# Buffers moved from the normalised tokens to the first projection's output in a windowed-attention and convolution kernel

## The chip, the cores and the metric

The kernel runs on one core of a Trainium2 chip. The metric is the device time of one launch in microseconds (us). Three executions of the kernel before took 3268.4, 3279.0 and 3279.86 us, with a median of 3279.0 us. One more execution was profiled; it took 3272.91 us, and its instructions span 3271.1 us.

## The reference, cut to what matters

There are two layers. The first is a windowed-attention block on a 4 x 128 x 128 x 128 image (batch, channels, rows, columns), followed by a depthwise convolution; the second is a pair of quantised 3x3 convolutions.

```python
reg = x[:, :, ih, iw]                       # 9 x 9 overlapping regions of 16 x 16 pixels, step 14
y = _ln(tok, ln1_g, ln1_b);  q, k, v = jnp.split(y @ w_qkv, 3, axis=-1)
attn = softmax(einsum(q, k) * hd ** -0.5);  o = einsum(attn, v)       # 4 heads of 32 channels
tok = o @ w_out + b_out + tok
xf = merged                                  # regions added back, divided by how often a pixel is covered
y = _ln(xf, ln2_g, ln2_b) @ w_p0 + b_p0      # first projection: 128 -> 256 channels, two halves of 128
ym = conv_general_dilated(y, dw_k, 5 x 5, feature_group_count=256)
ym = gelu(batchnorm(ym));  y = gelu(ym) @ w_p2 + b_p2 + xf
# second layer: quantise, conv3x3, batchnorm, quantise, conv3x3, batchnorm, + identity
```

## The kernel before, in words

**Bands.** The first layer is worked through in 36 bands: for each of the four images, nine rows of regions, with nine regions in a band. A band has 14 new rows of pixels (16 in an image's last band), cut into two chunks of 8 and 6 rows. Band number t runs `attention(t)` over its nine regions; I call the time of one region a slot, slot 0 to slot 8. TensorE, ScalarE, VectorE and SyncE follow the order in which the code records their instructions; only GpSimd's order is left to a scheduler.

**What goes beside the attention.** In each slot the main loop records the scores of region j, the values of region j-1, and between them four lists of side steps that `beside(t)` hands out. Three kinds of side work run:

- `ln1_chunks`, for the next band: normalise two chunks of input pixels (chunks a1 and a2). Its steps are squares, variance, deviation, spread, second (steps 0 to 4) and four projections to queries and keys (steps 5 to 8, line 483).
- `post_chunks`, for the band before: output projection (steps 0 and 1, line 535), the second layer norm (steps 2 to 6) and four first projections (steps 7 to 10: both halves of the channels for each half of the chunk, line 551). Its chunks are b1 and b2. Each first projection reads normalised tokens `xn` on TensorE, is evicted by ScalarE with its bias into a tile `y` (line 556), and is stored to the DRAM tensor `y_d` in runs of 256 bytes.
- `conv_steps`, from band 10 on: the depthwise convolution of an image that is complete, one step at a time, reading `y_d` into `u` tiles and writing `cv_d` (lines 590, 623, 637).

**Buffers.** `xnp` (line 181) holds three tiles of normalised tokens, 4 KB in each partition. The spread step broadcasts the reciprocal deviations from DRAM into such a tile (`xn<-row`, line 401, on SyncE's DMA queue), the second step multiplies it by the tokens on VectorE (line 411), and the projections read it. `y2t` (line 194) holds two tiles of 2 KB for each half of the channels; a first projection takes the front tile of its half's list and puts it at the end, so ScalarE can write it only when the store issued two projections of that half earlier has landed.

**Order of transfers.** Nearly all transfers are issued from SyncE's queue in the recorded order. A store is recorded one step after the step that made it.

**Slots and lists.** From band 10 on, b1's four first projections stand in slot 8 and b2's four in slot 0 of the next band (the list `left`). In bands 0 to 9, where there is no convolution, a table `full` (line 929; nine entries, one for each slot, with `f` the list left over from the band before) spreads them otherwise: two in slot 8, three in slot 0 and three in slot 1 of the next band; chunk a2's last two key and query projections stand in slot 7. After the last band a tail finishes the last image: `beside(T)` runs the remaining chunks one after the other, and `conv_rest` the remaining convolution.

A second copy of both layers with a safer softmax stands behind a flag; the profiled execution does not enter it.

Of the kernel before, what the change touches and what calls it, by code (L numbers as in the profile page):

```python
# [8 lines left out]
F32 = mybir.dt.float32  # L9
# [5 lines left out]
P = 128  # L15
# [6 lines left out]
RB = 4  # L22
# [10 lines left out]
CW = P // 2  # L33
# [13 lines left out]
def layers(  # L47
# [52 lines left out]
    def vector(v, name):  # L100
        n = v.shape[0] // P
        t = const.tile([P, n], F32, name=name)
        nc.sync.dma_start(out=t, in_=v.rearrange("(h p) -> p h", p=P))
        return t
# [16 lines left out]
    g1, b1 = vector(ln1_g, "g1"), vector(ln1_b, "b1")  # L121
# [3 lines left out]
    g2, b2 = vector(ln2_g, "g2"), vector(ln2_b, "b2")  # L125
# [7 lines left out]
    with (  # L133
# [21 lines left out]
        for w in (wqkv, wp0.rearrange("p h m -> p (h m)")):  # L155
            n = w.shape[1]
# [18 lines left out]
    with ExitStack() as actx:  # L175
        pool = lambda name, bufs, **k: actx.enter_context(
            tc.tile_pool(name=f"{name}_{tag}", bufs=bufs, **k)
        )
        rp, op = pool("rp", 2), pool("op", 2)
        y2p = pool("y2p", 1)  # L180
        work, dev, xnp, xfp = pool("work", 1), pool("dev", 2), pool("xnp", 3), pool("xfp", 2)
        rowp = pool("rowp", 4, space=bass.MemoryType.DRAM)
        small = pool("small", 6)
        ps_s, ps_o, ps_m = (pool(n, k, space=PSUM) for n, k in (("ps_s", 1), ("ps_o", 1), ("ps_m", 3)))
# [3 lines left out]
        pool = lambda name, bufs: bctx.enter_context(tc.tile_pool(name=f"{name}_{tag}", bufs=bufs))  # L188
# [2 lines left out]
        att, attn_t, attn_v = pool("att", 2 if safe else 4), pool("attn_t", 2), pool("attn_v", 2)  # L191


        y2t = [[y2p.tile([P, RB, 2, CW], F32, name=f"y2_{h}{n}") for n in range(2)] for h in range(2)]

        stores = []
        xb, xr, yr, qs, kr, ob = {}, {}, {}, {}, {}, {}
# [264 lines left out]
        def ln1_chunks(t, sel=None):  # L462

            chunks = []
            for at, (r, n) in enumerate(row_blocks(t)):
                held = {}
                squares, variance, deviation, spread, scaled = normalise(
                    lambda r=r, n=n: xb[t, r][:, : n * P], n * P, sel
                )

                def second(r=r, n=n, at=at, held=held, scaled=scaled):
                    held["xn"] = scaled()
                    load_ahead(t, at)
                    for hh in range(2):
                        nc.gpsimd.tensor_copy(
                            yr[t][:, :, r + hh * n // 2 : r + (hh + 1) * n // 2, :],
                            windows(held["xn"][hh], n // 2),
                        )

                def project(m, hh, r=r, n=n // 2, held=held):  # L480
                    r = r + hh * n
                    pm = ps_m.tile([P, 512], F32, name="pm")
                    nc.tensor.matmul(  # L483
                        pm[:, : n * P], wqkv[:, m * P : (m + 1) * P], held["xn"][hh],
                        start=True, stop=True,
                    )
                    if m:
                        nc.scalar.copy(kr[t][:, :, r : r + n, :], windows(pm, n))
                    else:
                        nc.scalar.activation(  # L490
                            rows_of(qs[t], r, n), pm[:, : n * P], AF.Identity, bias=qb
                        )

                chunks.append(
                    [squares, variance, deviation, spread, second]
                    + [lambda p=project, m=m, hh=hh: p(m, hh) for hh in range(2) for m in range(2)]
                )
            return chunks
# [15 lines left out]
        def fetch(t, n):  # L514

            xr[t, n] = load_rows(rp, "xr", t, *finished(t)[n])
# [353 lines left out]
        def beside(t, sel=None):  # L870

            one = list(early) if t else ln1_chunks(1)
            early[:] = ln1_chunks(t + 2) if t + 2 < T else []
            two = post_chunks(t - 1, sel) if t else []
            had = len(todo)
            if t >= 2:
                b, i = bands[t - 2]
                if i == NR - 1 and b < B - 1:  # L880
                    todo.extend(conv_steps(b))
                    share[0] = NR if b < B - 2 else 5
                elif b == B - 1 and i == 4:
                    todo.extend(conv_steps(B - 1))
                    share[0] = 2
                elif b == B - 1 and i == 6:
                    todo.extend(conv_steps(B))
                    share[0] = 1

            fresh = len(todo) > had  # L890
            n = len(todo) // share[0] if fresh else -(-len(todo) // max(share[0], 1))
            conv = [todo.pop(0) for _ in range(n)]
            share[0] -= 1
            a1, a2 = one if one else ([None] * 9,) * 2
            b1, b2 = two if two else ([None] * 11,) * 2
            if t == T:
                return [
                    *conv, *left, *b1[:2], *b2[:2], b1[2], b1[3], b2[2], b2[3], b1[4], b2[4], b1[5], b2[5],
                    b1[6], *b1[7:], b2[6], *b2[7:],
                ]  # L900


            c = [[] for _ in range(NR)]
            d = [[] for _ in range(NR)]
            twice = len(conv) > NR
            for j in sorted((1, 3, 5, 7, 8, 4, 6, 2, 0)[: len(conv)]):
                c[j] = [conv.pop(0)]
                d[j] = [conv.pop(0)] if twice and j and conv else []
            x1 = lambda: fetch(t, 0)
            x2 = lambda: fetch(t, 1)  # L910
            f, left[:] = list(left), b2[7:]
            s1 = early[0][0] if early else None
            plan = [
                ([a1[1]], [], f, [*c[0], a1[2]]),
                ([], [a1[3], *c[1]], [], [a2[0]]),
                ([a2[1]], [a1[4]], b1[:2], [*c[2], a2[2]]),
                ([], [a2[3], *c[3]], [], [b1[2]]),
                ([b1[3]], [a2[4]], [*a1[5:], *b2[:2]], [*c[4], b1[4]]),
                ([], [b1[5], *c[5]], [], [b2[2]]),
                ([b2[3]], [b1[6]], a2[5:], [*c[6], b2[4]]),  # L920
                ([], [b2[5], x1, *c[7]], [], []),
                ([], [b2[6], x2], b1[7:], [*c[8], s1]),
            ]
            if t == 0:
                plan[0] = ([], [], [], [*c[0], *a1[:3]])
            if t <= NR:

                left[:] = [*b1[9:], *b2[7:]]
                full = (f[:3], f[3:], b1[:2], a1[5:7], a1[7:], b2[:2], a2[5:7], a2[7:], b1[7:9])
                plan = [(one, two, w, four) for (one, two, three, four), w in zip(plan, full)]  # L930
            return [(one, two, three, four + d[j]) for j, (one, two, three, four) in enumerate(plan)]

# [8 lines left out]
        todo, share, left, early = [], [0], [], []  # L941
# [14 lines left out]
        with nullcontext() if safe else tc.manual_schedule(engines=MANUAL):  # L956
# [5 lines left out]
            for t in range(T):  # L962
                flush(len(stores))
                scores, halves, values_in, values = attention(t)
                if t + 1 < T:
                    ln1_begin(t + 1)
                for j, side in enumerate(beside(t)):
                    scores(j)
                    if last:
                        last()  # L970
                    run(side[0])
                    halves(j)
                    if j == 0 and t:
                        post_begin(t - 1)
                    run(side[1])
                    if j % 2 == 0:
                        values_in(j)
                    run(side[2])
                    run(side[3])
                    last = lambda j=j, values=values: values(j)  # L980
# [9 lines left out]
            flush(len(stores))  # L990
            rest = conv_rest(len(units) - 1, pools[0], pools[0], pools[1])
            run(beside(T, selector(pools[0].tile([P, 4 * P], F32, name="sel"))))
            flush(len(stores))
            rest()
# [337 lines left out]
def conv_seq_kernel(tc: tile.TileContext, *args: bass.AP):  # L1332
    nc = tc.nc
    with tc.tile_pool(name="flag", bufs=1) as fp:
        flag = fp.tile([1, 1], mybir.dt.int32, name="flag")
        layers(tc, False, flag, *args)


        large = nc.values_load(flag[0:1, 0:1])
        with tc.If(large > 0):  # L1340
            layers(tc, True, flag, *args)
# [34 lines left out]
```

## Time and profile before

| quantity | value |
|---|---|
| median of three runs | 3279.0 us |
| profiled execution | 3272.91 us |
| its span | 3271.1 us |
| TensorE busy | 3100.5 us, 95% of the span |
| VectorE busy | 2019.6 us, 62% |
| ScalarE busy | 1990.9 us, 61% |
| GpSimd busy | 837.5 us, 26% |
| DMA queue of SyncE | 75.6% of 16 engines' span |

The share of busy time is an average over the whole kernel; how far one engine waits for another is seen in the waits of a stretch. TensorE's busy time also contains matmuls that run at a lower clock. I number the bands by the first score matmul of every ninth slot: band 10 begins at 513.3 us, band 28 at 1557.8 us, band 29 at 1622.7 us, and the last band at 2098.3 us. The tail lies from about 2206 to 2335 us, and the second layer after it.

### The profile page before, as it was taken

How to read it: one execution, taken by the hardware profiler on the slowest of the kernel's cores; microseconds unless marked ns; L12 is line 12 of the kernel's file. 1: busy time of each engine (PE TensorE's matmuls, PEld its weight loads, DVE VectorE, ACT ScalarE, POOL GpSimd, SP SyncE). 2: the span in 40 equal slices, each digit the busy share in tenths (PEclk: the TensorE clock that was granted, in tenths of full speed). 3: DMA queues.
4: the chain of work that ended last, by engine and by line, in shares of the span. 5: the costliest groups of instructions: out<-in, count | busy, mean ns of one | idle time of the engine just before them, and what ended most of it. 6: DMA issues, size and time to landing. Idle time of an engine off the chain costs nothing.

```text
span 3271.1 us, 75716 instructions
## 1 busy us (share of the span) xinstructions
PE 3100.5 (95%) x30954; PEld 1550.6 (47%) x30954; DVE 2019.6 (62%) x3249; ACT 1990.9 (61%) x2654; POOL 837.5 (26%) x1058
## 2 busy tenths in 40 slices
PE   8999999999999999999999998886899999999998
PEld 4555554454444544444444445554444444444343
DVE  5877887766766667676655565442455555666543
ACT  5777776777776776777656564532467777333443
POOL 3444443333333333333322232211111111000000
PEclk9999999999999999999999998876799999999999
DMA  3555677888886788886899989857899999452398
GB/s 81 150 165 158 170 186 182 193 208 198 212 197 164 182 202 205 201 211 164 194 204 206 206 196 204 195 158 191 260 356 357 358 360 295 148 166 66 105 359 309
DMA packets 809827, 680.65 MB, mean 208 GB/s; under 512 B 580918, under 2 KB 695935, under 8 KB 809471
## 3 DMA queue, kind: packets, MB, share of 16 engines
q1 hardware_dynamic: 798879, 669.17, 75.6%
q8 instruction: 247, 4.05, 0.5%
q0 software_dynamic: 1024, 3.93, 0.5%
q10 hardware_dynamic: 9568, 2.61, 0.4%
q14 instruction: 109, 0.89, 0.1%
HBM read 408.72 MB, written 270.79 MB: 208 GB/s over the span
## 4 chain that ended last, share of the span: by engine, by line
PE 79%; DMA 7%; ACT 4%; issue 4%; DVE 3%; SPq 2%; POOL 0%; ACTq 0%; DVEq 0%; POOLq 0%
PE pc L1150 19%; PE pm L590 9%; PE sc L773 9%; PE po L836 8%; PE pb L1208 7%; PE pm L483 7%; PE pm L551 5%; PE pm L759 4%; PE po L844 4%; PE pm L367 3%; PE pm L535 3%; DMA y_d<-y 2%; ACT pt L781 1%; DMA u<-y_d 1%; DMA xn<-row 1%
## 5 line engine op out<-in xcount | busy, mean ns | idle before, releaser
L856 DVE RECIPROCAL rd<-po 128x256 f32<-128x256 f32 x324 | 569.2, 1757 | 462.1 <-PE po L844 459.3
L1150 PE MATMUL pc<-q,wq 128*128 128x512 fp8e4 x3168 | 702.1, 381 | 14.3 <-DVE q L1162 14.3
L781 ACT ACTIVATE pt<-sc 128x1024 f32<-128x1024 f32 x648 | 628.1, 1024 | 133.6 <-PE sc L773 69.1
L791 POOL TENSOR_TENSOR sm<-pt 128x512 f32<-128x512 f32 x324 | 413.1, 1275 | 1059.3 <-ACT pt L781 735.4
L1150 PEld LDWEIGHTS <-wq 128*128 128x128 fp8e4 x3168 | 309.1, 98 | 417.7 <-issue 50.3
L773 PE MATMUL sc<-q,kr 32*128 32x256 f32 x5184 | 404.6, 415 | 18.5 <-ACT pt L781 18.3
L590 PE MATMUL pm<-u,w 40*32 40x504 f32 (+5 forms) x7680 | 370.3, 506 | 32.7 <-DMA u<-y_d 21.0
L773 PEld LDWEIGHTS sc<-q,kr 32*128 32x128 f32 x5184 | 250.0, 191 | 258.6 <-issue 166.9
L836 PE MATMUL po<-pt,v 128*32 128x256 f32 x5184 | 361.2, 398 | 6.8 <-DVE part L860 5.5
L637 ACT COPY c<-pm 128x512 f32<-128x512 f32 (+1 forms) x256 | 132.4, 563 | 264.1 <-PE pm L590 243.4
L551 PE MATMUL pm<-xn,wp 128*128 128x512 f32 (+1 forms) x576 | 249.7, 564 | 36.4 <-ACT y L556 35.6
L556 ACT ACTIVATE y<-pm,bp 128x512 f32<-128x512 f32 (+1 forms) x288 | 183.0, 641 | 149.7 <-DMA y_d<-y 88.3
L791 DVE TENSOR_TENSOR sm<-pt 128x512 f32<-128x512 f32 x324 | 243.6, 752 | 25.7 <-ACT pt L781 25.7
L483 PE MATMUL pm<-xn,wqkv 128*128 128x512 f32 (+1 forms) x576 | 248.5, 560 | 2.7 <-ACT v L764 2.0
L590 PEld LDWEIGHTS pm<-u,w 40*32 40x32 f32 x7680 | 148.5, 113 | 213.1 <-issue 154.1
L641 DVE BATCH_NORM_STATS2 st<-c 128x6 f32<-128x512 f32 (+2 forms) x320 | 160.7, 550 | 132.2 <-ACT c L637 131.7
L1208 PE MATMUL pb<-cv,wp 128*128 128x512 f32 x512 | 232.9, 599 | 7.1 <-ACT cv L1199 7.1
L836 PEld LDWEIGHTS po<-pt,v 128*32 128x32 f32 x5184 | 139.7, 111 | 180.6 <-issue 105.6
L844 PE MATMUL po<-sm,ones 128*32 128x256 f32 x2592 | 206.3, 389 | 1.2 <-issue 1.2
L1158 DVE BATCH_NORM_STATS2 st<-pc 128x6 f32<-128x512 f32 x256 | 165.6, 689 | 67.5 <-PE pc L1150 67.5
L759 PE MATMUL pm<-wqkv,yr 128*128 128x128 f32 x1296 | 193.1, 290 | 1.3 <-ACT c L637 1.3
L759 PEld LDWEIGHTS pm<-wqkv,yr 128*128 128x128 f32 x1296 | 158.7, 191 | 69.9 <-issue 44.4
(157 smaller groups left out, 3445.4 us busy)
## 6 DMA issues: line engine op xcount, KB each, us to landing
cv<-cv_d SPq DMA_DIRECT2D x64, 1024.0 KB
u<-y_d SPq DMA_DIRECT2D x234, 256.0 KB
cv_d<-c SPq DMA_DIRECT2D x192, 256.0 KB
y_d<-y SPq DMA_DIRECT2D x160, 256.0 KB
xn<-row SPq DMA_DIRECT2D x76, 512.0 KB
xfl<-xf_d SPq DMA_DIRECT2D x64, 512.0 KB
id_d<-y SPq DMA_DIRECT2D x64, 512.0 KB
idt<-id_d SPq DMA_DIRECT2D x64, 512.0 KB
```

What stands on the lines that cost most here:

```text
L483: nc.tensor.matmul(pm[:, : n * P], wqkv[:, m * P : (m + 1) * P], held["xn"][hh], start=True, stop=True,)
L551: nc.tensor.matmul(pm[:, : n * P], wp0[:, h, :], held["xn"][hh], start=True, stop=True)
L590: nc.tensor.matmul(outs[half][32 * q : 32 * q + 32, j, :, a:z], wt[hs, s, c, :], ut[hs, :, c, a + s - 1 : z + s - 1], start=(s == 1), stop ...
L759: nc.tensor.matmul(pv[:, m, c, :], region(yr, j + m)[:, c * P : (c + 1) * P], wqkv[:, 2 * P :], start=True, stop=True,)
L773: nc.tensor.matmul(sc[h // 2][:, h % 2, kc, :].rearrange("p (r c) -> p r c", c=RS), region(kr, j)[hs, kc * P : (kc + 1) * P], queries(j, h ...
L781: nc.scalar.activation(pt, sc[p], AF.Exp)
L791: add(sm, pt[:, :, 0, :], pt[:, :, 1, :], ALU.add)
L836: nc.tensor.matmul(po[hs, 0, :], v[:, kc, hs], pt[h // 2][:, h % 2, kc, :], start=(kc == 0), stop=(kc == 1),)
L844: nc.tensor.matmul(po[hs, 1, :], ones, sm[h // 2][:, h % 2, :], start=True, stop=True)
L856: nc.vector.reciprocal(rd, po[:, 1, :])
L1150: nc.tensor.matmul(pc[:, h], w[:, t, :], q1[b][:, r + dy : r + dy + RB, dx : dx + P], start=(t == 0), stop=(t == 8),)
L1208: nc.tensor.matmul(pb[:, m], wp2[:, h, :], cv[:, h, px], start=(h == 0), stop=(h == 1))
```

## The change

The change moves 4 KB of on-chip memory from one pool to another: `xnp` has two tiles instead of three, and `y2t` three tiles for each half of the channels instead of two. To fit this, the table of the first ten bands is rewritten: b1's four first projections all stand in slot 8, two of b2's in slot 0 and two in slot 1 of the next band, and chunk a2's four projections all in slot 6, so that slot 7 has no such work. The list `left` is no longer set apart for these bands. Nothing is computed that was not computed before.

```diff
-        work, dev, xnp, xfp = pool("work", 1), pool("dev", 2), pool("xnp", 3), pool("xfp", 2)
+        work, dev, xnp, xfp = pool("work", 1), pool("dev", 2), pool("xnp", 2), pool("xfp", 2)
...
-        y2t = [[y2p.tile([P, RB, 2, CW], F32, name=f"y2_{h}{n}") for n in range(2)] for h in range(2)]
+        y2t = [[y2p.tile([P, RB, 2, CW], F32, name=f"y2_{h}{n}") for n in range(3)] for h in range(2)]
...
             if t <= NR:
 
-                left[:] = [*b1[9:], *b2[7:]]
-                full = (f[:3], f[3:], b1[:2], a1[5:7], a1[7:], b2[:2], a2[5:7], a2[7:], b1[7:9])
+                full = (f[:2], f[2:], b1[:2], a1[5:7], a1[7:], b2[:2], a2[5:], [], b1[7:])
                 plan = [(one, two, w, four) for (one, two, three, four), w in zip(plan, full)]
```

## The prediction

> **What bounds the kernel now.** I read the page first, then the waits of the stretches that its slices set apart, then the timelines of one band. On the page, TensorE is busy for 95% of the span and carries 79% of the chain that ended last. Time is therefore saved only where TensorE itself waits, or where it runs slowly. One wait in the page's groups belongs to the tile that the change gives a third buffer:
>
> ```profile
> PE 79%; DMA 7%; ACT 4%; issue 4%; DVE 3%; SPq 2%; POOL 0%; ACTq 0%; DVEq 0%; POOLq 0%
> L556 ACT ACTIVATE y<-pm,bp 128x512 f32<-128x512 f32 (+1 forms) x288 | 183.0, 641 | 149.7 <-DMA y_d<-y 88.3
> ```
>
> ScalarE idles 88.3 us until stores of `y` have landed. By stretch, the waits put 0.7 us of this into bands 0 to 9, 17.3 us into bands 11 to 26, 53.0 us into bands 29 to 35 and 16.4 us into the tail. Band 30 shows the large kind (timelines of ScalarE, TensorE and SyncE; start, duration, instruction, and in brackets the idle time before it):
>
> ```profile
> 1704.88 0.59 ACT L764 COPY v<-pm 128x512 f32<-128x512 f32 x1 [0.32 <-PE pm L759]
> 1710.01 0.58 ACT L556 ACTIVATE y<-pm,bp 128x384 f32<-128x384 f32 x1 [4.54 <-DMA y_d<-y]
> 1710.90 0.58 ACT L556 ACTIVATE y<-pm,bp 128x384 f32<-128x384 f32 x1 [0.31 <-DMA y_d<-y]
> 1711.92 0.58 ACT L556 ACTIVATE y<-pm,bp 128x384 f32<-128x384 f32 x1 [0.44 <-DMA y_d<-y]
> 1716.53 0.58 ACT L556 ACTIVATE y<-pm,bp 128x384 f32<-128x384 f32 x1 [4.03 <-DMA y_d<-y]
> 1718.59 1.94 ACT L781 ACTIVATE pt<-sc 128x1024 f32<-128x1024 f32 x2 [0.63 <-ACT rstd L382]
> ```
> ```profile
> 1704.68 2.40 PE L551 MATMUL pm<-xn,wp 128*128 128x384 f32 x6
> 1710.64 1.65 PE L551 MATMUL pm<-xn,wp 128*128 128x384 f32 x2 [3.56 <-ACT y L556]
> 1712.22 2.09 PE L773 MATMUL sc<-q,kr 32*128 32x256 f32 x16
> ```
> ```profile
> 1702.16 3.40 SPq L435 DMA_DIRECT2D xr<-in_x_dram  x1
> 1705.65 3.23 SPq L421 DMA_DIRECT2D y_d<-y  x3
> 1708.98 1.97 SPq L623 DMA_DIRECT2D u<-y_d  x4
> 1711.04 0.39 SPq L421 DMA_DIRECT2D y_d<-y  x1
> 1711.53 3.88 SPq L421 DMA_DIRECT2D cv_d<-c  x2
> 1715.50 3.05 SPq L421 DMA_DIRECT2D y_d<-y  x4
> ```
>
> The four `y` of slot 0 want the tiles that slot 8 filled from 1695.14 to 1698.4, but SyncE, held up by slow issues, sent those stores only at 1705.65 and 1711.04. ScalarE waits in order, so the exponentials of slot 1 start at 1718.59, and TensorE, out of `pm` tiles, idles 3.56 us and then runs 16 score matmuls in 2.09 us, which took 1.15 us elsewhere. Slots 0 and 1 show the price: 19.4 us here, 12.5 us in band 18, which has the same work and no such wait (columns: length, busy time of the five engines, granted clock, DMA share, GB/s):
>
> ```profile
> 1700.30:1719.70 19.40, 15.81 (x168) 7.25 (x160) 7.41 (x10) 8.97 (x15) 3.47 (x6) 0.82 1.08 226
> 978.00:990.50 12.50, 12.47 (x161) 6.32 (x160) 6.42 (x9) 9.45 (x14) 4.78 (x6) 1.00 0.65 135
> ```
>
> **What the Trainium skill says.** "Perfetto Trace Analysis", section Optimization Strategy: the same gap repeating on the engine that should be saturated can mean too few buffers for the next tile. The trace agrees: the gap returns in slot 0 of bands 29, 30, 31, 32, 34 and 35. "TensorE: Matmul & The Clock Gate", Part 1: after about 3.4 us without work the array falls to half clock until it has been busy as long. The 3.56 us gap, the 2.09 us for 1.15 us and the 0.82 above agree. "DMA: Bandwidth & Descriptors", Anatomy of one DMA, gives about 2.0 us fixed before a completion is seen; the trace has 4.36 us from the issue at 1705.65 to ScalarE's start at 1710.01, with the DMA share at 1.08.
>
> **The change part by part.** All sums are against the profiled 3272.9 us (span 3271.1); the median of the runs shown is 6.1 us higher, and I carry differences over to it.
>
> *Third `y` tile, bands 29 to 35.* From band 10 on no step moves. Slot 0's first two `y` take tiles free since the band before; the third waits for slot 8's first store and the fourth for its second. The landings that released the first and second `y` now release the third and fourth, so the fourth can start about 0.6 us after the old second. The old second and fourth starts are 1632.88/1640.29, 1710.90/1716.53, 1785.50/1793.24, 1864.02/1869.68, 2018.02/2026.34 and 2106.35/2108.19 (band 33 has no wait). Fourth minus second minus 0.6 gives 6.8 + 5.0 + 7.1 + 5.1 + 7.7 + 1.2 = 33 us. Also, slot 2 of bands 29, 31 and 32 took 8.6, 9.5 and 8.6 us against 6.1 in bands 12 to 15, since TensorE had idled 1.3 to 3.4 us before it and was at low clock; this gives back 7 us. TensorE no longer idles 3.5 us, because the four L551 find their `pm` tiles and slot 1's scores and values follow while the third `y` waits. Of these 40 us I return 12: SyncE hands out slot 0's stores at 1715.50 to 1718.55 as before, so it gains some 2 us where TensorE gains 5, and the next row load and `u` loads are late by the rest, 2 us in each of bands 29 to 32 and 34, and 2 us for band 35, where TensorE waited 5.28 us for `u` after it. Net -28 us; bounds -40 and -8.
>
> *Bands 11 to 27.* In slot 0 the first `y` waited 0.9 to 2.1 us in eleven bands and the second 1.1 us in band 25; the third and fourth need slot 8's stores 1.8 us later, when they have landed. Slot 0 took 7.5 to 8.8 us there against 7.3 in bands 11, 18 and 20. The excesses over 7.3, bands 12 to 17 and 21 to 26, are 0.2, 1.0, 0.4, 0.5, 0.4, 0.9, 1.5, 0.5, 1.0, 1.4, 0.0 and 0.3, sum 8. Net -8; bounds -10 and -3.
>
> *Tail.* The fifth `y` of the last eight waits 15.72 us behind a store queued after large loads. With three tiles the fifth and sixth go at once, the seventh and eighth at the old times of the fifth and sixth (2253.90, 2254.81). The last `y` moves from 2256.76 to about 2254.9, and the last `u` loads with it. SyncE had spent until then on the earlier stores. Net -2; bounds -3 and 0.
>
> *The rewritten table, bands 0 to 10.* Counts stay; places move. TensorE there waits for almost nothing, so balance counts. Slot 0 loses two first projections of 512 columns and gains one of 384, slot 1 loses one of 384, and slot 8 gains the two. With 0.86 us from one to the next (evictions at 1695.14, 1696.00 and on) slots 0 and 1 become 1.7 us shorter. Slot 6 gains two L483 of 384 columns (x4, 1.56 us) and slot 7 loses them. But an empty slot 7 can't shrink as far: ScalarE's exponentials, already 1 us late at slot 7 because of the deviation steps before them, hold the next scores. Bands 18 and 27 have an empty slot 7 and four projections in slot 8: 3.2 and 7.5 us. Now slots 6, 7, 8 take 7.6 + 4.0 + 4.9 = 16.5 us; then, by those rows, 9.1 + 3.2 + 7.5 = 19.8. By TensorE's work alone they would take 18.2. I take 19.3 (+2.8), because VectorE also has a 1.1 us copy for the convolution's weights in these slots. Eight bands at 2.8 - 1.7 give +9, band 1 (whose slots 0 and 1 lose nothing) +2.8, band 0 +0.5, and band 10, whose slot 0 held six projections, -2.4: +10; bounds 0 and +16.
>
> *Two `xn` tiles.* Each row load would now wait for the tile two loads back instead of three. In bands 11 to 33 the load is issued at least 2.98 us after TensorE's last read of that tile (least for b2 in slot 7; 3.15 for b1, 11 for a1, 14 for a2), because it waits for its own row anyway. So it costs nothing. The new table keeps this: a2 is read out in slot 6 and b1 in slot 8. Without that cover SyncE would stop in front of the convolution's loads; bounds 0 and +3.
>
> The sum is -28 - 8 - 2 + 10 + 0 = -28 us, hence 3245 us against the profile and 3251 us against the median.
>
> **The rivals.** (A) *The DMA engines give the gain back.* Bands 29 to 32 have DMA shares of 0.93, 0.92, 0.90 and 0.92; a band shorter by 7 of 75 us needs 1.0. For it: SyncE's slow issues. Against it: short stretches reach 1.08 and more, there are idle pockets at 1746 and 1764 us, and TensorE waits for `u` only 6.4 us between 1622 and 2100. Then bands 29 to 35 give -8 and the total is -8: 3271 us. (B) *Nothing is returned and the clock stays up*: -40 - 10 - 3 + 5, or -48: 3231 us. (C) *Slower.* One cause: the pile-up in slots 6 to 8 of the first ten bands, with ScalarE late for slot 7's exponentials. It decides once it outweighs the 38 us of the other parts, at over 4.2 us for each of nine bands; at 6 us (slot 7's exponentials late by the four evictions of slot 6, 2.3 us, and slot 8's again by its four, 2.7 us, on top of 1.0) it gives +54 - 38 = +16: 3295 us. For it: ScalarE already starts them late (357.91 us for scores done at 357.0). Against it: bands 18 and 27 show 10.7 us for the two slots with the same order. That the third tile changes nothing is excluded by the first two `y` of slot 0.
>
> **How the numbers follow.** My forecast has 0.60, A 0.20, B 0.10, C 0.10. The likeliest is 3251 us, its own range 3236 to 3263. A change under 0.5% (16.4 us) can hardly be told from none with runs that differ by 11 us. Faster by more: the forecast nearly whole, B, and a little of A, 0.70; within: the rest of A and the edge of the forecast, 0.20; slower: C, 0.10. The range takes in A, most of B and the spread of runs: 3229 to 3276 us.
>
> **What would show it.** In the profile after, ScalarE's wait for `y_d` should fall from 88 to some 45 us, its longest still in the tail; slots 0 and 1 of bands 29 to 32 should take 13 to 16 us and show no 2.09 us scores; slot 0 of bands 12 to 26 should take 7.3 us. In bands 2 to 9 slots 7 and 8 should take 3.2 and 7 us and the band 50 instead of 49. I am wrong if bands 29 to 35 wait as long for `xn<-row` or `u`, if SyncE's row loads wait for a first or second projection, or if bands 2 to 9 grow by over 3 us each.

## The result and the profile after

The changed kernel took 3289.57 us (median of nine runs, 3284.43 to 3301.51) and the kernel before 3275.3 us beside it (nine runs, 3260.93 to 3284.77). The ratio is 1.005, with a 95% interval of 1.0036 to 1.0065: slower by 0.5%, where I had forecast 0.9% faster, and above the range that I gave (3229 to 3276 us). The profiled execution took 3294.24 us and its span is 3292.4 us, 21.3 us more than before. The two lines of the page that I showed of before read as follows after the change (the chain of work that ended last, and the group of the `y` evictions):

```profile
PE 80%; DMA 6%; ACT 5%; issue 4%; DVE 4%; SPq 1%; POOL 0%; ACTq 0%; DVEq 0%; POOLq 0%
L556 ACT ACTIVATE y<-pm,bp 128x512 f32<-128x512 f32 (+1 forms) x288 | 183.5, 641 | 100.9 <-PE pm L551 55.3
```

ScalarE's idle time before `y` fell from 149.7 to 100.9 us, and the stores of `y` no longer end most of it. So the third tile did what it says. The waits of the whole kernel after the change show what rose (who waits, for what; us in total, times, longest):

```profile
DVE xn L411 <- DMA xn<-row: 78.9, 40, 7.7
ACT y L556 <- DMA y_d<-y: 40.0, 20, 12.3
PE pm L590 <- DVE xf L536: 22.7, 8, 7.3
PE pm L590 <- ACT y L556: 6.7, 1, 6.7
```

The same four before:

```profile
DVE xn L411 <- DMA xn<-row: 52.8, 29, 5.3
ACT y L556 <- DMA y_d<-y: 88.3, 62, 15.7
PE pm L590 <- DVE xf L536: 2.7, 3, 1.6
PE pm L590 <- ACT y L556: 2.0, 2, 1.8
```

The wait for `y_d` fell from 88.3 to 40.0 us. VectorE's wait for row loads rose from 52.8 to 78.9 us, and a wait of TensorE's that was 2.7 us in all, for VectorE's eviction `xf`, is now 22.7 us. It lies in bands 28 to 35, where the `y` waits had been.

Slots 0 and 1 of band 30 show the gain, slots 3 and 4 the loss (after the change, by window: length, busy time of the five engines, granted clock, DMA share, GB/s):

```profile
1709.51:1723.50 13.99, 13.52 (x168) 6.46 (x160) 7.47 (x10) 8.84 (x15) 3.46 (x5) 1.00 1.03 220
1732.10:1757.10 25.00, 21.80 (x213) 8.38 (x212) 13.02 (x22) 10.56 (x16) 6.40 (x8) 0.90 0.82 199
```

Before, slots 0 and 1 took 19.4 us at a clock of 0.82. Slots 3 and 4 of band 30 took 17.3 us before at full clock:

```profile
1726.60:1743.90 17.30, 17.30 (x213) 8.43 (x212) 12.46 (x21) 9.67 (x14) 6.43 (x8) 1.00 0.96 224
```

In slot 0 of the same band ScalarE's timeline after the change is as the prediction drew it: two `y` go at once, the third and fourth wait for the stores of slot 8's tiles, and TensorE has gone on meanwhile:

```profile
1714.73 0.58 ACT L556 ACTIVATE y<-pm,bp 128x384 f32<-128x384 f32 x1
1715.67 0.58 ACT L556 ACTIVATE y<-pm,bp 128x384 f32<-128x384 f32 x1 [0.36 <-PE pm L551]
1719.67 0.58 ACT L556 ACTIVATE y<-pm,bp 128x384 f32<-128x384 f32 x1 [3.42 <-DMA y_d<-y]
1720.46 0.58 ACT L556 ACTIVATE y<-pm,bp 128x384 f32<-128x384 f32 x1 [0.20 <-DMA y_d<-y]
```

The loss comes in slots 3 and 4. SyncE's, VectorE's and TensorE's timelines of slot 4:

```profile
1739.07 3.94 SPq L435 DMA_DIRECT2D xt<-in_x_dram  x1
1743.11 0.38 SPq L421 DMA_DIRECT2D xf_d<-xf  x1
1743.59 0.38 SPq L401 DMA_DIRECT2D xn<-row  x1
```
```profile
1744.45 0.68 DVE L791 TENSOR_TENSOR sm<-pt 128x512 f32<-128x512 f32 x1
1750.35 1.03 DVE L411 TENSOR_TENSOR xn<-xn,xt 128x384 f32<-128x384 f32 x2 [5.22 <-DMA xn<-row]
1751.30 1.14 DVE L536 SCALAR_TENSOR_TENSOR xf<-pm,bo,xr 128x384 f32<-128x384 f32 x2
```
```profile
1748.19 1.06 PE L590 MATMUL pm<-u,w 40*32 40x512 f32 x8
1751.96 5.29 PE L590 MATMUL pm<-u,w 40*32 40x512 f32 x40 [2.71 <-DVE xf L536]
1757.18 2.09 PE L773 MATMUL sc<-q,kr 32*128 32x256 f32 x16
```

Chunk a2's row load is issued at 1743.59. VectorE's multiplication of a2 waits 5.22 us for it, and the eviction `xf` of b2, whose matmuls ended at about 1748.2, stands behind it in VectorE's order. It holds the `pm` tiles, so TensorE stops 2.71 us in the convolution, then runs it at a low clock (5.29 us for 40 matmuls; the same 40 took 2.75 us in slot 3), and the 2.09 us scores are back at slot 5.

To see where the 21.3 us came from I cut the profiled executions by the first score matmul of a band (us; the last stretch ends with the first matmul of the second projection; what is left differs by 1.3 us between the two):

| stretch | before | after | difference |
|---|---|---|---|
| bands 0 to 10 | 546.5 | 563.1 | +16.6 |
| bands 11 to 27 | 984.5 | 972.7 | -11.8 |
| bands 28 to 34 | 540.5 | 564.5 | +24.0 |
| band 35 and tail | 230.8 | 224.6 | -6.2 |

Of the +24.0, 17.1 lie in band 34 alone. Each column is a single execution, while the medians differ by 14.3 us. In three profiles with two `y` tiles and none of the moves tried below (the kernel before, the table alone, two `xn` tiles alone) bands 28 to 34 took 540.5, 543.9 and 546.1 us, so a difference of some 6 us in this stretch of one profile can be spread.

### The profile page after: what moved, and what is told of

Same layout as the page of the kernel before. It is cut to its first block, busy times and chain, and to the rows that moved or that the text cites. A ratio compares the mean times of both kernels' runs of the same rounds, so it can differ in the third digit from the quotient of the medians.

```text
span 3292.4 us, 75653 instructions
## 1 busy us (share of the span) xinstructions
PE 3114.7 (95%) x30954; PEld 1551.9 (47%) x30954; DVE 2021.3 (61%) x3249; ACT 1994.9 (61%) x2654; POOL 837.1 (25%) x1058
## 4 chain that ended last, share of the span: by engine, by line
PE 80%; DMA 6%; ACT 5%; issue 4%; DVE 4%; SPq 1%; POOL 0%; ACTq 0%; DVEq 0%; POOLq 0%
PE pc L1149 19%; PE pm L590 10%; PE sc L773 9%; PE po L836 9%; PE pm L483 6%; PE pm L551 6%; PE pb L1207 6%; PE pm L759 5%; PE po L844 4%; PE pm L367 3%; PE pm L535 2%; ACT pt L781 2%; DMA xn<-row 1%; DMA w<-dw_d 1%; DMA u<-y_d 1%
## 5 line engine op out<-in xcount | busy, mean ns | idle before, releaser
L1149 PE MATMUL pc<-q,wq 128*128 128x512 fp8e4 x3168 | 701.8, 381 | 14.3 <-DVE q L1161 14.3
L590 PE MATMUL pm<-u,w 40*32 40x504 f32 (+5 forms) x7680 | 387.0, 514 | 63.2 <-DMA u<-y_d 24.5
L773 PE MATMUL sc<-q,kr 32*128 32x256 f32 x5184 | 411.1, 415 | 20.2 <-ACT pt L781 20.1
L791 DVE TENSOR_TENSOR sm<-pt 128x512 f32<-128x512 f32 x324 | 241.4, 745 | 19.8 <-ACT pt L781 19.6
L556 ACT ACTIVATE y<-pm,bp 128x512 f32<-128x512 f32 (+1 forms) x288 | 183.5, 641 | 100.9 <-PE pm L551 55.3
L551 PE MATMUL pm<-xn,wp 128*128 128x512 f32 (+1 forms) x576 | 243.1, 554 | 0.9
```

The source lines that it names most:

```text
L551: nc.tensor.matmul(pm[:, : n * P], wp0[:, h, :], held["xn"][hh], start=True, stop=True)
L590: nc.tensor.matmul(outs[half][32 * q : 32 * q + 32, j, :, a:z], wt[hs, s, c, :], ut[hs, :, c, a + s - 1 : z + s - 1], start=(s == 1), stop ...
L773: nc.tensor.matmul(sc[h // 2][:, h % 2, kc, :].rearrange("p (r c) -> p r c", c=RS), region(kr, j)[hs, kc * P : (kc + 1) * P], queries(j, h ...
L791: add(sm, pt[:, :, 0, :], pt[:, :, 1, :], ALU.add)
L1149: nc.tensor.matmul(pc[:, h], w[:, t, :], q1[b][:, r + dy : r + dy + RB, dx : dx + P], start=(t == 0), stop=(t == 8),)
```

## The experiments

The change has three parts: the table, the second `xn` tile, the third `y` tile. The first batch takes them apart, all against one kernel before (median 3268.61 us of 30 runs).

**The table alone** (three `xn` and two `y` tiles kept, the new `full`).

```diff
-                left[:] = [*b1[9:], *b2[7:]]
-                full = (f[:3], f[3:], b1[:2], a1[5:7], a1[7:], b2[:2], a2[5:7], a2[7:], b1[7:9])
+                full = (f[:2], f[2:], b1[:2], a1[5:7], a1[7:], b2[:2], a2[5:], [], b1[7:])
```

> The new table of the first ten bands, with three xn tiles and two y tiles as before. Theory (the table costs, and the third y tile's gain in bands 28 to 35 is taken back by later waits): bands 0 to 10 take 17 us more than before, as in the changed kernel, bands 11 to 35 as before; about +17 us in all. Rival (the two xn tiles are what costs): bands 0 to 10 take at most 5 us more, and the whole within 5 us of before.

Measured: 3287.88 us (nine runs), ratio 1.0047 (1.0029 to 1.0065). Bands 0 to 10 took 562.8 us. By the medians the whole slowdown is here.

**The buffers alone** (two `xn`, three `y`, old table) and **two xn tiles alone** (`y` at two).

```diff
-        work, dev, xnp, xfp = pool("work", 1), pool("dev", 2), pool("xnp", 3), pool("xfp", 2)
+        work, dev, xnp, xfp = pool("work", 1), pool("dev", 2), pool("xnp", 2), pool("xfp", 2)
...
-        y2t = [[y2p.tile([P, RB, 2, CW], F32, name=f"y2_{h}{n}") for n in range(2)] for h in range(2)]
+        y2t = [[y2p.tile([P, RB, 2, CW], F32, name=f"y2_{h}{n}") for n in range(3)] for h in range(2)]
```

> Two xn tiles and three y tiles, with the table of before. Theory: bands 0 to 10 within 4 us of before, bands 11 to 27 about 11 us shorter, bands 28 to 35 and the tail not shorter (0 to +18 us), so -11 to +7 us in all. Rival (two xn tiles cost): bands 0 to 10 or bands 28 to 35 at least 10 us longer than before although no table was changed, so +5 us or more in all. My first forecast's step (a third y tile saves 28 us in bands 29 to 35): -38 us.

> Two xn tiles, two y tiles, the table of before: only the removed xn tile is left of the change. Theory: within 4 us of before in every part. Rival: at least 10 us slower, with SyncE's row loads waiting for first projections or for query and key projections.

Measured: buffers alone 3269.11 us (14 runs), ratio 1.0000 (0.9989 to 1.0012); two `xn` tiles alone 3267.26 us (14 runs), ratio 0.9995 (0.9983 to 1.0008). The second `xn` tile costs nothing, and the third `y` tile, from which I expected 38 us, brings nothing either. In the profile with buffers alone bands 28 to 34 took 547.1 us against 540.5, so nothing was gained there. Band 29 shows SyncE, VectorE and TensorE in the same relation as above, here with chunk a1 in slot 3:

```profile
1636.62 3.85 SPq L421 DMA_DIRECT2D cv_d<-c  x2
1640.56 3.04 SPq L421 DMA_DIRECT2D y_d<-y  x4
1645.16 0.33 SPq L401 DMA_DIRECT2D xn<-row  x1
```
```profile
1649.75 1.29 DVE L411 TENSOR_TENSOR xn<-xn,xt 128x512 f32<-128x512 f32 x2 [7.45 <-DMA xn<-row]
1650.96 1.40 DVE L536 SCALAR_TENSOR_TENSOR xf<-pm,bo,xr 128x512 f32<-128x512 f32 x2
```
```profile
1651.76 5.29 PE L590 MATMUL pm<-u,w 40*32 40x512 f32 x40 [5.95 <-DVE xf L536]
1656.98 2.09 PE L773 MATMUL sc<-q,kr 32*128 32x256 f32 x16
```

The time at which a1's row load is issued tells why. Counted from the start of its band, it was issued after 21.8, 20.2, 22.5 and 19.8 us in bands 29 to 32 before, and after 23.0, 21.0, 21.5 and 19.2 us with buffers alone. SyncE did not come a microsecond earlier on the average. But slot 2, where VectorE's multiplication of a1 stands, ended 29.4, 26.3, 31.0 and 28.1 us after the start before, and 20.1, 22.0, 22.5 and 20.5 us with the third tile. Before, TensorE was late for other reasons and never waited for `xf` in these four bands; now TensorE is early and waits 14.1 us for it, because `xf` stands behind the wait for the row.

**The stores of `y` on ScalarE's queue**, in the changed kernel, so that they don't stand behind SyncE's loads.

```diff
-                    store(
-                        y2_d[b][row + 2 : row + n + 2, :, h * P : (h + 1) * P, :].rearrange(
+                    nc.scalar.dma_start(
+                        out=y2_d[b][row + 2 : row + n + 2, :, h * P : (h + 1) * P, :].rearrange(
```

> The changed kernel, with the stores of y issued from ScalarE's queue right after each y instead of from SyncE's. If the stores are late because SyncE's queue in its recorded order is late: ScalarE's waits for y_d fall from 40 us to under 10, slots 0 and 1 of bands 29 to 34 go to 12.5 us, and bands 28 to 35 take 20 us or more less than in the changed kernel; -15 us or better against it. If the DMA engines themselves are full there: the stores land no earlier, bands 28 to 35 stay within 8 us, and ScalarE pays 0.5 us for each issue.

Measured: 3331.79 us (five runs), ratio 1.0185 (1.0165 to 1.0205). Bands 28 to 34 took 541.1 us, 23 less than in the changed kernel (13 of them in band 34), but bands 0 to 10 and 11 to 27 took 585.0 and 1008.2 us, 57 us more together. ScalarE's timeline of the last two `y` of band 6's slot 8 shows the price:

```profile
385.37 0.69 ACT L556 ACTIVATE y<-pm,bp 128x512 f32<-128x512 f32 x1 [0.50 <-ACT y L556]
386.09 1.17 ACTq L561 DMA_DIRECT2D y_d<-y  x1
387.36 0.69 ACT L556 ACTIVATE y<-pm,bp 128x512 f32<-128x512 f32 x1 [1.30 <-DMA dw_d<-u]
388.08 1.31 ACTq L561 DMA_DIRECT2D y_d<-y  x1
389.44 1.06 ACT L361 ACTIVATE sq<-xt 128x1024 f32<-128x1024 f32 x1 [1.39 <-issue]
```

ScalarE issues a store in 0.4 to 1.3 us, and its next instruction waits until then. (For the wait of 1.30 us the view names a transfer, but the issue of 1.17 us, which had just ended, accounts for it.) Two evictions start 1.99 us apart where they were 0.86 us apart. Over bands 0 to 27 TensorE's waits for `sq`, which stands behind such issues, rose from 5.1 us in the changed kernel to 33.7 us.

The second batch (kernel before 3264.74 us, 12 runs) asks which part of the table costs, and whether the row load or the transfers' volume holds up bands 29 to 32.

**Slot 7 kept**: the changed kernel, with a2's last projections back in slot 7.

```diff
-                full = (f[:2], f[2:], b1[:2], a1[5:7], a1[7:], b2[:2], a2[5:], [], b1[7:])
+                full = (f[:2], f[2:], b1[:2], a1[5:7], a1[7:], b2[:2], a2[5:7], a2[7:], b1[7:])
```

> The changed kernel, but chunk a2's last two query and key projections stay in slot 7, as before; b1's four first projections stand in slot 8, as in the change. If the emptied slot 7 is what the table costs: slot 7 takes 4.0 us again, slot 8 about 6.7, slot 6 7.0 to 8.1, bands 0 to 10 within 4 us of before and the whole within 5 us of before. If four projections in slot 8 are what costs: slot 8 stays at 7.5 us, bands 0 to 10 stay 12 us or more above before, and the whole +11 us or more.

Measured: 3277.41 us (five runs), ratio 1.0048 (1.0024 to 1.0072), no better than the changed kernel. Its profiled execution, 3266.95 us, was its fastest, and so says little of the median: there bands 0 to 10 took 555.3 us, and over bands 1 to 9 slots 6 to 8 took 166.7 us, against 149.3 before and 175.5 after the change. So in that profile the emptied slot 7 is about a third of what slots 6 to 8 lost, and the rest goes with the four `y` of slot 8; by the medians the part of slot 7 is not shown.

**The row load early**: from band 10 on chunk a1's deviation and spread stand in slot 0, with buffers alone and in the kernel before.

```diff
-                ([a1[1]], [], f, [*c[0], a1[2]]),
-                ([], [a1[3], *c[1]], [], [a2[0]]),
+                ([a1[1]], [], [a1[2], *f[:2], a1[3], *f[2:]], c[0]),
+                ([], c[1], [], [a2[0]]),
```

> Two xn tiles and three y tiles with the table of before, and from band 10 on chunk a1's deviation runs on ScalarE ahead of slot 0's four first projections, and its row load is recorded after the second of them instead of in slot 1. If the saved y wait is lost because that load stands behind slot 0's stores in SyncE's order: VectorE's waits of 5 to 8 us in slot 2 or 3 of bands 29 to 32 fall under 2 us, slots 3 and 4 of these bands go from 26 to 29 us to under 21, and bands 28 to 35 take 20 us or more less than with the buffers alone. If the DMA engines are simply full from slot 7 to slot 3: another wait takes the place (for u, or for the store of y), and bands 28 to 35 stay within 8 us of the buffers alone.

> The same move of the row load in the kernel before, with three xn and two y tiles. The y wait of slot 0 stays in place here (12 us for slots 0 and 1 more than 12.5 us per band), and it hides the row load, so the move gains nothing: within 5 us of before. If it is faster by more than 8 us, the row load cost time there too.

Measured: with buffers alone 3279.84 us (five runs), ratio 1.0047 (1.0033 to 1.0061); in the kernel before 3278.55 us (five runs), ratio 1.0038 (1.0025 to 1.0052). The edit has a cost that I had not expected: in bands 11 to 27 both took 997.4 us, 21 us more than buffers alone, because slot 0 is 8.7 instead of 7.3 us: ScalarE's deviation step with its store now stands ahead of the first `y` (in band 15 that `y` starts 7.2 instead of 5.2 us after the band's start). In bands 28 to 34 it took 541.2 us with three tiles, 5.9 less than buffers alone, and 535.0 with two tiles, 5.5 less than before. Slot 3 of bands 29 to 32 fell from 48.1 to 34.9 us with three tiles, but slot 4 rose from 55.4 to 65.6. It doesn't bring out a gain of the third tile.

**One row of `xr`**: buffers alone, and from band 28 on each load of the residual brings one row, with the rest filled on GpSimd. The kernel leaves out that part of the residual.

```diff
-            xr[t, n] = load_rows(rp, "xr", t, *finished(t)[n])
+            r, rows = finished(t)[n]
+            xr[t, n] = load_rows(rp, "xr", t, r, rows if t < 28 else 1)
```

> Buffers alone, but from band 28 on each load of the pixels for the residual (512 or 384 KB, in slots 7 and 8) brings one row in place of eight or six; the rest of the tile is filled with zeros on GpSimd. It leaves out part of the residual. If the traffic of slots 7 to 0 fills the DMA engines and so makes everything behind it late: the y waits in slot 0 or 1 of bands 29 to 34 and VectorE's waits for the row load fall by more than half, and bands 28 to 35 take 15 us or more less than with the buffers alone. If not the traffic but the order sets the lateness: less than 6 us.

Measured: 3255.6 us (four runs), ratio 0.9978 (0.9956 to 1.0). With less to carry, slots 0 to 2 of bands 29 to 32 became 9.4 us shorter than with buffers alone, but slots 3 and 4 became 3.5 us longer, and VectorE's wait for row loads from band 28 on even rose, from 54.2 to 64.5 us. Bands 28 to 34 became 8.6 us shorter, between the amounts that I had set for traffic and for order. That the order on VectorE holds TensorE is not changed by lighter transfers.

The third batch (kernel before 3265.37 us, 42 runs) therefore moves not the row load but what waits for it. One thing goes along that I had overlooked: the step with the multiplication also issues the load of the next band's pixels (`xt`, by `load_ahead`), so these edits change SyncE's order too. In band 30 a1's `xt` load went from 30.1 us after the band's start with buffers alone to 37.3 us. The two effects were not taken apart. Theory I: the gain is lost because evictions stand behind a multiplication that waits for its row. Theory II: what the transfers of a band can carry is used up, and each wait taken away returns at the next.

**The multiplication of a1 later**, from the middle of slot 2 to the end of slot 3, from band 10 on; with buffers alone and in the kernel before. A third kernel puts it at the front of slot 3's middle list.

```diff
+            if t > NR:
+                plan[2] = ([a2[1]], [], b1[:2], [*c[2], a2[2]])
+                plan[3] = ([], [a2[3], *c[3]], [], [b1[2], a1[4]])
```

> Buffers alone (xn 2, y 3, old table), and from band 10 on VectorE's multiplication of a1 by its reciprocal deviations stands at the end of slot 3 instead of in the middle of slot 2, so that b1's eviction `xf` no longer stands behind it. Theory I (in bands 29 to 32 the gain at slots 0 and 1 is lost because VectorE waits 3.7 to 7.5 us for the row load with `xf` queued behind it): TensorE's wait for `xf` falls from 21 us to under 8, slots 3 and 4 of bands 29 to 32 take 18 to 20 us instead of 24 to 29, bands 28 to 34 become 20 to 35 us shorter, bands 11 to 27 change by under 4 us, and the total is about 3240 us (ratio to before 0.990 to 0.994). Theory II (what the transfers can carry in a band is used up, so that each wait taken away returns at the next): slots 3 and 4 become shorter but slots 4 to 8 or the next slot 0 longer, bands 28 to 34 change by under 8 us, ratio 0.998 to 1.002.

> As the run before, but the multiplication stands at the front of slot 3's middle list, ahead of the convolution's step, about half a slot earlier. Theory I: `xf` is free of it here too, but VectorE may still wait 2 to 4 us for the row with the convolution's work behind it: 10 to 30 us shorter in bands 28 to 34, ratio 0.991 to 0.997. Theory II: under 8 us, ratio 0.998 to 1.002.

> The same move of the multiplication to the end of slot 3, in the kernel before (two y tiles, three xn tiles). Theory I: TensorE waits only 2.7 us for `xf` there, because it waits for `y` first and the row has landed by then, so the move is worth 0 to 4 us: ratio 0.998 to 1.001. Theory II: ratio 0.998 to 1.001 too; a gain of over 10 us here would mean that the place of the multiplication matters without the third tile, against Theory I.

Measured: 3256.93 us (22 runs), ratio 0.9974 (0.9963 to 0.9984); in the middle 3273.09 us (13 runs), ratio 1.0021 (1.0007 to 1.0034), with 554.6 us for bands 28 to 34, 7.5 more than buffers alone, where Theory I had 10 to 30 less; in the kernel before 3263.07 us (14 runs), ratio 0.9994 (0.9984 to 1.0003). Neither theory is met in full. Slot 3 of bands 29 to 32 fell from 48.1 to 20.9 us, as Theory I has it, but slot 4 rose from 55.4 to 71.5, and bands 28 to 34 became only 4.1 us shorter, as Theory II has it. VectorE's and TensorE's timelines of slot 4 of band 30 show why:

```profile
1725.95 1.03 DVE L411 TENSOR_TENSOR xn<-xn,xt 128x384 f32<-128x384 f32 x2 [5.52 <-DMA xn<-row]
1726.90 1.14 DVE L536 SCALAR_TENSOR_TENSOR xf<-pm,bo,xr 128x384 f32<-128x384 f32 x2
```
```profile
1727.57 4.81 PE L590 MATMUL pm<-u,w 40*32 40x512 f32 x40 [3.46 <-DVE xf L536]
1732.31 2.09 PE L773 MATMUL sc<-q,kr 32*128 32x256 f32 x16
```

It is the same wait with the next chunk: a2's multiplication, with b2's `xf` behind it. So the last batch (kernel before 3275.85 us, 19 runs) moves that one too.

**Both multiplications later**, a2's from slot 4 to the end of slot 5; with buffers alone and in the kernel before. Its `xt` load goes along here too, in band 30 from 43.4 to 59.9 us after the band's start.

```diff
+                plan[4] = ([b1[3]], [], [*a1[5:], *b2[:2]], [*c[4], b1[4]])
+                plan[5] = ([], [b1[5], *c[5]], [], [b2[2], a2[4]])
```

> The late multiplication of a1 at the end of slot 3 with buffers alone, and now a2's multiplication too, moved from the middle of slot 4 to the end of slot 5, so that b2's eviction `xf` no longer stands behind it. Theory I (evictions queued behind multiplications that wait for their row): in bands 29 to 32 slots 4 and 5, 71.5 and 30.1 us over the four bands in the run before, fall to 48 to 52 and 21 to 25 us, TensorE's wait for `xf` from 14 to under 4 us; bands 28 to 34 become another 15 to 30 us shorter, total 3227 to 3242 us, ratio to before 0.988 to 0.993. Theory II (the transfers of a band are the bound): the wait reappears in slots 5 to 8 or in the next slot 0, bands 28 to 34 change by under 8 us, ratio 0.996 to 0.999.

> Both moves in the kernel before (two y tiles). Theory I: the waits for the stores of `y` at slots 0 and 1 of bands 29 to 35 stay (48 us of ScalarE's idle time there), and the multiplications hold up nothing that TensorE waits for: ratio 0.997 to 1.001. If it gains as much as with three tiles, the third tile is worth nothing.

Measured: with buffers alone 3262.56 us (six runs), ratio 0.9966 (0.9954 to 0.9978); in the kernel before 3277.29 us (14 runs), ratio 1.0009 (0.9994 to 1.0025). TensorE no longer waits for `xf` in bands 28 to 34 (21.2 us with buffers alone). Its waits there with buffers alone and both moves:

```profile
PE pm L590 <- DMA u<-y_d: 17.8, 13, 3.6
PE pm L590 <- DMA cv_d<-c: 6.1, 5, 2.8
```

They are waits for the convolution's transfers: 6.7 us for `u` in the kernel before, 17.8 us now, 4.8 of them in bands 29 to 32. In slot 8 of band 32 the old wait shows a third time: VectorE's multiplication of b1 waits 7.74 us for its row, and TensorE stops 4.16 us for a VectorE instruction behind it. Bands 29 to 32, in us by groups of slots, show how the same time wanders:

| kernel | slots 0 to 2 | slots 3, 4 | slots 5 to 8 | sum |
|---|---|---|---|---|
| before | 114.8 | 69.2 | 118.8 | 302.9 |
| after | 88.0 | 101.8 | 118.6 | 308.4 |
| buffers alone | 85.1 | 103.5 | 116.8 | 305.5 |
| a1 later | 80.4 | 92.3 | 126.6 | 299.3 |
| both later | 81.2 | 69.2 | 146.2 | 296.7 |
| both later, two `y` tiles | 115.7 | 69.2 | 116.1 | 301.0 |

The third tile takes 30 us out of slots 0 to 2. With the old order 34 come back in slots 3 and 4; with both multiplications moved, 27 come back in slots 5 to 8. The same four bands as one window, before and with both moves:

```profile
1622.67:1925.55 302.88, 280.90 (x3305) 133.80 (x3297) 177.32 (x275) 177.96 (x274) 84.27 (x108) 0.94 0.92 205
```
```profile
1611.26:1907.94 296.68, 284.26 (x3305) 134.15 (x3297) 176.14 (x275) 178.76 (x274) 84.18 (x108) 0.94 0.92 210
```

The DMA share is 0.92 in both; the same bytes go through in 2% less time. Theory II's numbers (ratio 0.996 to 0.999, bands 28 to 34 within 8 us of the step before) hold for this last step. That fits a queue of transfers that sets the pace of these bands, but doesn't show it: with one row of `xr` the share was 0.88, and the four bands still took 299.5 us. Another order of issues was not tried, so whether the DMA engines, the order or the semaphores described at the end bind is open.

By the medians the version with buffers alone and both multiplications later, and the one with a1's alone, beat the kernel before, the first by 0.34% (0.22% to 0.46%). Without the third tile the same moves bring nothing (1.0009), so the tile is worth something once these steps stand later. Where the time is saved is not shown. In the profile with both moves, the fastest of its six runs, bands 28 to 34 took 543.4 us, no less than the 540.5 before; the shorter stretches are bands 11 to 27 (972.3 for 984.5), of which buffers alone already had 8.1 us, and band 35 with the tail (223.7 for 230.8).

## Why the prediction was wrong

**The third tile, bands 29 to 35 (forecast -28, of 40 gross).** In bands 29 to 32 the gross gain was right. Slots 0 and 1 there took 12.6, 14.1, 14.2 and 13.9 us (I said 13 to 16, no 2.09 us scores), and the wait for `y_d` fell to 40.0 us (I said 45). The step that failed is "Of these 40 us I return 12". I reckoned that SyncE gains some 2 us where TensorE gains 5. With buffers alone it gained nothing: the row load was issued 21.2 us after a band's start on the average, against 21.1 before. So not 12 us came back but all: bands 28 to 34 took 547.1 us, against 540.5 to 546.1 us with two tiles. I had named the row load as the next to be late, but not asked what stands behind the instruction that waits for it. That is `xf`, which holds TensorE's `pm` tiles; a stop of 2.7 us or 6 us costs at least another 3.5 us at the low clock (5.29 us of convolution for 2.75, 2.09 us of scores for 1.15). "TensorE waits for `u` only 6.4 us" was weak evidence against rival A, since TensorE was held up earlier in each band; with both multiplications moved it waited 17.8 us for `u` in bands 28 to 34. And what I called SyncE's slow issues are in part waits for semaphores (last section). Why SyncE gained nothing is not settled beyond that.

**Band 34.** In the changed kernel's profile it took 105.3 us against 88.2, which no step foresaw. ScalarE, TensorE and SyncE in its slot 0:

```profile
2037.37 0.58 ACT L556 ACTIVATE y<-pm,bp 128x384 f32<-128x384 f32 x1 [8.79 <-DMA y_d<-y]
```
```profile
2038.00 5.29 PE L590 MATMUL pm<-u,w 40*32 40x256 f32 x88 [6.74 <-ACT y L556]
```
```profile
2022.84 7.84 SPq L421 DMA_DIRECT2D cv_d<-c  x4
2031.33 4.86 SPq L421 DMA_DIRECT2D y_d<-y  x3
```

It is the wait for the stores of `y` again, two evictions later: SyncE spent 7.84 us on four other stores before it sent slot 8's, 6.3 of them waiting until the transfers that had last used the stores' semaphores had landed. Three tiles cover two evictions more, not a store that is 9 us late. Slot 0 of band 34 took over 21 us in three of the eight profiles with three `y` tiles and the stores on SyncE, and 10 to 12 in the others. It did so in one with two tiles as well (21.1 us, the row load early), so this part is neither in every execution nor the third tile's alone.

**Bands 11 to 27 (-8) and the tail (-2).** Right. Slot 0 took 7.3 us in fourteen of these bands and 7.6 to 8.0 in three; the stretch fell by 11.8 us after the change and by 8.1 with buffers alone. Band 35 and the tail fell by 6.2 and 4.5 us, more than I said, but this stretch ranged from 221.9 to 231.7 us in the profiles with two tiles.

**The rewritten table (+10, at most +16).** The mechanism was right, and a term was missing: slots 2 to 5, which I put at nothing. Over bands 1 to 9 slots 6 to 8 grew by 26.2 us (175.5 for 149.3), 2.9 for each band where I said 2.8; slots 7 and 8 took 3.1 and 7.5 us as in bands 18 and 27. Slots 0 and 1 gave 12.3, about what I said. But slots 2 to 5 grew by 4.7 us (4.2 with the table alone). With bands 0 and 10 the sum is +16.6, just over my upper bound. At the end of slot 6 and in slot 7 of band 6 after the change, ScalarE and then TensorE:

```profile
367.66 0.58 ACT L490 ACTIVATE q<-pm,qb 128x384 f32<-128x384 f32 x1
368.30 0.52 ACT L488 COPY kr<-pm 128x432 f32<-128x432 f32 x1
368.72 0.46 ACT L381 ACTIVATE rstd<-rstd,eps_t 128x192 f32<-128x192 f32 x1
369.21 0.36 ACT L382 ACTIVATE rstd<-rstd 128x192 f32<-128x192 f32 x1
370.19 1.94 ACT L781 ACTIVATE pt<-sc 128x1024 f32<-128x1024 f32 x2 [0.61 <-ACT rstd L382]
```
```profile
368.20 1.16 PE L773 MATMUL sc<-q,kr 32*128 32x256 f32 x16
371.26 0.70 PE L773 MATMUL sc<-q,kr 32*128 32x256 f32 x4 [0.48 <-ACT pt L781]
```

The scores of slot 7 end at 369.36, and their exponentials start at 370.19, behind two evictions moved into slot 6 and the deviation steps. Slot 7 has no projection left to fill the time, so the scores of slot 8 stop for the exponentials. This is rival C's mechanism, but at 2.9 us for each band and not 6. The table is the only part that costs time in the medians: 1.0047 alone, 1.0000 for the buffers, 1.005 together.

**Two xn tiles (0).** Right: 0.9995 (0.9983 to 1.0008).

**The rivals.** Rival A, the gain given back in bands 29 to 35, came true, at 0.20 in my chances. But A kept 8 us of the gain in bands 29 to 35, and even with the table at its upper bound its sum would be -8 - 8 - 2 + 16 = -2 us. The medians rose by 14.3 us: besides the table, nothing was left of those 8 us, and the 8 and 2 us of the other stretches, which the profile with buffers alone has, don't show in its median (1.0000). "Perfetto Trace Analysis", section Optimization Strategy, which I read as support for more buffers, speaks of what such a gap can mean. Here the gap did go away with the buffers, and the time did not: 1.0000.

## What to carry to other kernels

Before a wait is counted as saved, ask when the next transfer that the same engine needs is issued, counted from the start of the repeating stretch; if a queue of transfers sets that time and not the engine, the saved time waits there. Look also at what stands in order behind the instruction that will wait: moving two multiplications behind an eviction, and the loads that their steps issue with them, took the third tile from 0.0% to a gain of 0.3% by the medians. And a step that frees memory for a buffer has its own price, which must be counted over all the repetitions of the place that pays it: here 0.5% for a table of ten bands.

## What the runs showed of the hardware that I had not expected

In this program the transfers of SyncE's and ScalarE's queues count up eight semaphores in turn, and before each issue the engine waits on the one that it will use, that is, until the transfer eight back has landed. With buffers alone in band 29 SyncE was free at 1637.00 us, but issued its next store at 1640.11, when the store of a1's row that ScalarE had issued at 1633.62, of four packets only, had landed (1640.05, 6.4 us after its issue; the DMA share of slots 0 to 2 was 0.95). After the stores of `y` it was free at 1643.61, but issued the load of a1's row at 1645.16, when the store of a2's row, issued by ScalarE at 1642.62, had landed (1645.08). So one slow transfer holds up both queues, whatever they carry.

Summed over bands 29 to 32, SyncE waited in this way until ScalarE's row stores had landed, ahead of transfers that don't read the row, 33.0 us in the kernel before, 53.9 us with buffers alone and 38.3 us with both multiplications later. So some of what the third tile freed may have come back here, a rival to both theories that no run tests: the row stores were not put elsewhere. How much of the 57 us that stores on ScalarE's queue cost in bands 0 to 27 comes from the semaphores is not shown either.

A short stop was followed by the low clock. In band 30 of the changed kernel the trace has TensorE idle for 2.71 us, and 40 matmuls that took 2.75 us in slot 3 took 5.29 us after it. "TensorE: Matmul & The Clock Gate", Part 1, gives about 3.4 us without work. The start of the gap is modelled: the eight matmuls ahead of it are drawn with 1.06 us, where 40 in 2.75 us would make it 0.55, so the gap may have been up to 3.2 us long, and the trace doesn't decide against the page.
